# A four-layer state-space network: who scales the inflows of the scans, who forms the C products, and when the next chunk is prepared

## The chip, the core and the metric

The kernel runs on one core of a Trainium2 chip. Five engines have a queue of instructions each and run it in order: TensorE (PE; its weight loads are shown as PEld) multiplies and transposes into PSUM, VectorE (DVE), ScalarE (ACT) and GpSimd (POOL) work element by element, and SyncE (SP) issues the transfers. Engines wait for each other by semaphores. The metric is the time of one execution on the device in microseconds; lower is better.

## The reference

Four layers are applied to four images of 64 x 64 pixels with 192 channels. Each normalizes its input by groups, projects it, convolves it, and runs selective scans over it. Layer 0 ("a" in the kernel) has four directions over single rows or columns, each 64 long; layer 1 ("b") one direction, layer 2 ("c") four with 192 channels, layer 3 ("d") four with 384, all over the whole image of 4096 positions. The core of all is the recurrence, here from layer 3:

```python
def step(hst, inp):
    d, bm, cm, uu = inp
    dA = jnp.exp(d[..., None] * A[None])
    dBu = (d * uu)[..., None] * bm[:, :, None, :]
    hst = dA * hst + dBu
    y = jnp.einsum('bkdn,bkn->bkd', hst, cm)
    return (hst, y)
...
delta = jax.nn.softplus(dts + dt_projs_bias[None, :, :, None])
ys = ys + xs * Ds.reshape(K, D_INNER)[None, :, :, None]
```

There are 16 states n for every channel d. Four things are computed for each: the decay dA, the inflow dBu (delta times u, times B), the scan itself, and the product with C, which is summed over the states. All arithmetic is in 32-bit floats.

## The kernel before

**Tiling.** `scans` (from line 313 on) handles all scans of one layer. The sequence is cut into chunks of T = 512 positions. A chunk has 384 channels as nb = 3 blocks of 128 partitions; the 16 states are taken as 8 pairs j of NT = 2. One tile is one pair of one block, 128 x 1024 elements, so a chunk has 24 tiles and each tile has one scan on VectorE (line 695). In c the rows and columns are worked on side by side in one set of blocks (`ways` = 2). For an image a has 32 chunks, b 8, c 16 and d 32.

**Steps.** The loop at line 800 runs over all tiles, one tile a step s, and writes the order of each engine's queue by hand: `keep` (line 437) ties each instruction behind the one before it on its engine. In step s the queues get: the decays of tile s+3 (two exponentials on ScalarE, line 631; NF = 4 buffers in a, b, d and 3 in c), the inflow of tile s+1, the scalings due in this step, the scan of tile s, loads for later tiles, the C product of tile s-1 on GpSimd or of tile s on VectorE (line 710), and the sum of tile s-3 (or s-1 after VectorE) by transposing matmuls into one PSUM bank a block (`total`, line 750). So the inflow of tile s+1 stands in TensorE's queue in front of the totals and of the preparation of step s.

**Inflows.** There are four ways to form dBu. "p": GpSimd multiplies du by a broadcast B (line 637), and the decay lies in PSUM. The other three work on du transposed (duT, positions on partitions, where B is one number a partition). "t": ScalarE scales duT by B (line 658), TensorE transposes the result into PSUM (line 674). "g": the same with GpSimd scaling (line 651). "d": TensorE multiplies duT by a diagonal matrix that holds B (line 670); the matrix is written element by element into memory and loaded again as D. `WAYS` gives order and way of the pairs: in a three pairs d, four t, one g; in b and d two d, two g, four t; in c p and t in turn. PSUM holds two inflow tiles ("ps"); a buffer is free when the scan has read it, or, where VectorE makes the C product in place, after that product.

**C products.** `PRODUCTS` says for each of a chunk's 24 tiles whether GpSimd ("p", the scan writes to an h buffer in SBUF) or VectorE ("d", the scan writes over its input) forms the product.

**Scalings.** The eight scalings of a pair (two states, four blocks of 128 positions) are laid over the steps ahead of its first tile, 6 steps for t and 9 for g (lines 771 to 777), into three buffers for t and two for g, one buffer a state.

**Preparation.** While a chunk is scanned the next is prepared at the steps of the table `at` (line 552): px (projection to dt, B, C on TensorE, steps 3 to 5), dbl (copy by ScalarE, step 6), pd and pre (delta's projection and bias by block, in one PSUM bank in turn, steps 7 to 11), softplus (12), du on GpSimd (13), the transposes of du and their copies (15 to 20). A `brought` part adds the state carried over a chunk's border through f (lines 501, 680) in b, c and d. In d and the second pass of c the sum of the directions so far is loaded as "far" at step 12 and added by TensorE with the last totals (line 757).

## Time and profile before

Three runs took 30,927.73, 30,931.62 (the median) and 30,941.47 us. The profiled execution took 30,932.74 us with a span of 30,931.0 us from the first to the last instruction; the granted TensorE clock was 0.945 of full speed on the mean.

| engine | busy us | share of the span | instructions |
|---|---|---|---|
| TensorE, matmuls | 26,989.1 | 87% | 183,112 |
| TensorE, weight loads | 21,403.1 | 69% | 183,112 |
| VectorE | 24,057.7 | 78% | 14,749 |
| ScalarE | 22,386.5 | 72% | 42,791 |
| GpSimd | 22,167.3 | 72% | 13,662 |

The DMA engines were busy for 35.5% of the span with the kernel's own queue. In the profile a group of instructions is shown as "line engine operation out<-in shapes xcount | busy us, mean ns of one | idle time of the engine just before them, and what ended it"; names end in the layer's letter. A line of waits reads "engine, tile and line <- what released it: us in total, times, longest". Busy time of TensorE counts modelled ends of pipelined matmuls, so a busy TensorE need not be at its peak. A releaser is inferred from the last semaphore, and with several waits it can be another than the one named. The four images repeat the same pattern, so one image's layers show the stages.

### The profile page before, as it was taken

Reading aid. Unit: us, or ns where it says so; the run is one execution under the profiler, and the core shown is the slowest. Engines: PE = TensorE matmul, PEld = TensorE weight load, DVE = VectorE, ACT = ScalarE, POOL = GpSimd, SP = SyncE. Lnnn points to the kernel's source line nnn. Section 1 sums busy time; section 2 is a strip of 40 time slices with the busy share of each in tenths; the row PEclk is TensorE's granted clock in tenths of the full one; section 3 lists DMA queues with packets and bytes.
Section 4 is the critical chain, followed back from the end, with each engine's and each line's share of the span. In section 5 each row is a group of like instructions: output and inputs, shape, how many; then the busy total and the mean of one; then the engine's idle time right before and its main releaser. Section 6 shows DMA issues by size and latency. Waiting matters only on the chain. (4 is left out here: it accounts for less than half of the span.)

```text
span 30931.0 us, 474683 instructions
## 1 busy us (share of the span) xinstructions
PE 26989.1 (87%) x183112; PEld 21403.1 (69%) x183112; DVE 24057.7 (78%) x14749; ACT 22386.5 (72%) x42791; POOL 22167.3 (72%) x13662
## 2 busy tenths in 40 slices
PE   8998877999899986799989988779998998877998
PEld 6885655887688565588768856558876885655886
DVE  7884788887788478888778847888877884788887
ACT  6883686886688368688668836868866883686886
POOL 4882686887588268688758826868875882696897
PEclk9999988999999998899999999889999999988999
DMA  3332343333333234333333323433333332343333
GB/s 114 108 109 80 88 116 100 92 99 102 108 109 108 81 87 115 102 92 100 102 108 108 108 81 88 115 102 92 100 103 108 109 109 78 89 115 101 91 100 100
DMA packets 2029473, 3108.17 MB, mean 100 GB/s; under 512 B 902744, under 2 KB 1350600, under 8 KB 2019272
## 3 DMA queue, kind: packets, MB, share of 16 engines
q1 hardware_dynamic: 2027208, 3077.78, 35.5%
q8 instruction: 1444, 23.66, 0.3%
q14 instruction: 821, 6.73, 0.1%
HBM read 2590.78 MB, written 486.54 MB: 99 GB/s over the span
## 5 line engine op out<-in xcount | busy, mean ns | idle before, releaser
L710 POOL TENSOR_TENSOR c_a<-h_a,C_a 128x1024 f32<-128x1024 f32 x2688 | 6334.4, 2373 | 1555.4 <-DVE h_a L695 874.0
L695 DVE TENSOR_TENSOR_SCAN h_d<-dAs_d,carry_d,ut_d 128x1024 f32<-128x1024 f32 x2688 | 6198.1, 2336 | 1417.1 <-PE ut_d L670 854.1
L710 POOL TENSOR_TENSOR c_d<-h_d,C_d 128x1024 f32<-128x1024 f32 x2688 | 6390.9, 2384 | 1040.0 <-PE py_d L750 454.8
L695 DVE TENSOR_TENSOR_SCAN h_a<-dAs_a,ut_a 128x1024 f32<-128x1024 f32 x2688 | 6008.0, 2273 | 1042.7 <-POOL dut_a L651 301.0
L631 ACT ACTIVATE dAs_a<-delta_a,A_a 128x504 f32<-128x504 f32 x6144 | 4039.0, 707 | 1083.8 <-DVE h_a L695 772.7
L631 ACT ACTIVATE dAs_d<-delta_d,A_d 128x512 f32<-128x512 f32 (+1 forms) x6144 | 4093.1, 715 | 653.6 <-DVE h_d L695 496.4
L750 PE MATMUL py_a<-ident,c_a 128*128 128x128 f32 x24576 | 3195.0, 277 | 11.1 <-DVE c_a L710 11.1
L750 PE MATMUL py_d<-ident,c_d 128*128 128x128 f32 x24576 | 3153.3, 273 | 11.2 <-DVE c_d L710 11.2
L674 PE MATMUL ut_d<-ident,dut_d 128*128 128x128 f32 x18432 | 2893.3, 281 | 306.2 <-DVE c_d L710 133.3
L674 PEld LDWEIGHTS ut_d<-ident,dut_d 128*128 128x128 f32 x18432 | 2201.2, 152 | 1173.7 <-DVE h_d L695 374.9
L750 PEld LDWEIGHTS py_a<-ident,c_a 128*128 128x128 f32 x24576 | 2840.3, 143 | 12.1 <-DVE c_a L710 12.1
L750 PEld LDWEIGHTS py_d<-ident,c_d 128*128 128x128 f32 x24576 | 2793.1, 142 | 66.2 <-issue 53.8
L750 PE MATMUL py_c<-ident,c_c 128*128 128x128 f32 x12288 | 1915.8, 313 | 936.3 <-DVE c_c L710 689.7
L674 PE MATMUL ut_a<-ident,dut_a 128*128 128x128 f32 x15360 | 2148.9, 283 | 564.9 <-ACT dut_a L658 387.2
L674 PEld LDWEIGHTS ut_a<-ident,dut_a 128*128 128x128 f32 x15360 | 1739.2, 144 | 1087.6 <-ACT dut_a L658 419.9
L750 PEld LDWEIGHTS py_c<-ident,c_c 128*128 128x128 f32 x12288 | 1666.9, 163 | 1142.0 <-DVE c_c L710 669.9
L670 PEld LDWEIGHTS ut_a<-D_a,duT_a 128*128 128x128 f32 x18432 | 2144.9, 192 | 365.2 <-DVE h_a L695 253.3
L670 PE MATMUL ut_a<-D_a,duT_a 128*128 128x128 f32 x18432 | 2280.0, 278 | 103.7 <-DVE c_a L710 75.9
L710 POOL TENSOR_TENSOR c_c<-h_c,C_c 128x1024 f32<-128x1024 f32 x960 | 2254.8, 2364 | 152.9 <-issue 106.8
L658 ACT ACTIVATE dut_d<-duT_d,BT_d 128x384 f32<-128x384 f32 x4096 | 2321.0, 603 | 0.7 <-PE ut_d L674 0.7
L658 ACT ACTIVATE dut_a<-duT_a,BT_a 128x384 f32<-128x384 f32 x4096 | 2316.2, 601 | 0.9 <-PE ut_a L674 0.7
L695 DVE TENSOR_TENSOR_SCAN h_c<-dAs_c,carry_c,ut_c 128x1024 f32<-128x1024 f32 x768 | 1766.9, 2335 | 167.5 <-PE ut_c L674 157.5
(374 smaller groups left out, 54166.5 us busy)
## 6 DMA issues: line engine op xcount, KB each, us to landing
C_a<-bc_a SPq DMA_DIRECT2D x1024, 512.0 KB
C_d<-bc_d SPq DMA_DIRECT2D x1024, 512.0 KB
C_c<-bc_c SPq DMA_DIRECT2D x1024, 256.0 KB
D_a<-dg SPq DMA_DIRECT2D x384, 512.0 KB
C_b<-bc_b SPq DMA_DIRECT2D x256, 512.0 KB
B_c<-bc_c SPq DMA_DIRECT2D x512, 256.0 KB
D_d<-dg SPq DMA_DIRECT2D x256, 512.0 KB
xd_a<-xo_a SPq DMA_DIRECT2D x48, 2048.0 KB
```

The source lines that it names most:

```text
L631: keep(nc.scalar.activation(out, delta, AF.Exp, scale=o.A[:, t.b, k : k + 1]))
L658: keep(nc.scalar.activation(o[:, :, g, :], i[:, :, g, :], AF.Copy, scale=c.BT[:, q, g, n : n + 1]))
L670: keep(nc.tensor.matmul(out, t.c.duT[:, q, blk], t.c.D[t.j][:, n, q, :], start=q == 0, stop=stop))
L674: keep(nc.tensor.matmul(out, t.c.scaled[t.n0 + n][:, q, blk], self.ident, start=q == 0, stop=stop, is_transpose=True,))
L695: keep(nc.vector.tensor_tensor_scan(hf, af, uf, initial, ALU.mult, ALU.add))
L710: keep(engine.tensor_tensor(t.cm, t.h, t.c.C[t.j], ALU.mult))
L750: keep(nc.tensor.matmul(c.py[b][:, q, :], t.cm[:, n, q * 128 : (q + 1) * 128], self.ident[:P, :P], start=first, stop=last and q == TB - 1 ...
```

## The change

All inflows take the form with duT; the way "p" with its loads of B, its u tiles and its decays in PSUM is gone. In a five pairs are scaled by ScalarE, two by GpSimd and one is diagonal; in b and d five and three, with no diagonal; in c four and four. The pairs now run in their natural order 0 to 7. GpSimd's scaling of c works on half-blocks, 128 x 192 elements, two instructions for each state and block of positions. VectorE forms 4 C products a chunk in a, 5 in b and d, 8 in c. The scalings of a chunk are spread evenly from step -7 (t) or -6 (g) of a chunk to two steps before the last such pair is used, with four buffers for t, and three (four in c) for g. The decays have four buffers in all layers, h five. The table of the preparation is packed into steps 0 to 17, and the sum so far is loaded into the tile that the result will be stored from. Only C goes through memory to be broadcast.

```diff
-WAYS = {
-    0: ((2, "d"), (0, "t"), (3, "d"), (1, "t"), (5, "g"), (6, "t"), (4, "d"), (7, "t")),
-    1: ((3, "d"), (0, "t"), (2, "g"), (1, "t"), (4, "d"), (6, "t"), (5, "g"), (7, "t")),
-    2: tuple((j, "pt"[j % 2]) for j in range(8)),
-}
-DIAGS = {0: (4, 6), 1: (6, 4)}
-ROW = 3328
+WAYS = {0: "tgttgttd", 1: "tgttgttg", 2: "tgtgtgtg"}
+DIAGS = {0: (14, 2)}
+ROW = 1280
...
-PRODUCTS = {1: "pppppppdpppppppdpppppppd", 2: "dpdpppdpdpppdddpppdpdppp"}
+PRODUCTS = {
+    0: "pppppdpppppdpppppdpppppd", 1: "ppppdppppdppppdppppdpppd", 2: "ppdppdppdppdppdppdppdppd",
+}
+FIRST_SCALE = {"t": -7, "g": -6}
...
-        HB = 5 if ways == 1 else 4
-        DUT = {"t": 3, "g": 2}
-        AHEAD = {"t": 2 * nb, "g": 3 * nb}
...
-            c.bc = dp.tile([ways, 2 * NS, T], F32, tag="bc", bufs=3, name=f"bc_{c.key}")
+            c.bc = dp.tile([ways, NS, T], F32, tag="bc", bufs=3, name=f"bc_{c.key}")
             for g in range(ways):
-                k = g * (DR + 2 * NS) + DR
-                keep(nc.sync.dma_start(c.bc[g], c.dbl[k : k + 2 * NS, :]))
-            if ways == 1:
+                k = g * (DR + 2 * NS) + DR + NS
+                keep(nc.sync.dma_start(c.bc[g], c.dbl[k : k + NS, :]))
+            if kind in DIAGS:
...
-            c.du = sp.tile([P, nb, T], F32, tag="du", bufs=ways, name=f"du_{c.key}")
+            c.du = sp.tile([P, nb, T], F32, tag="du", bufs=1, name=f"du_{c.key}")
...
-            0: [p_dir], 3: [p_px(0)], 4: [p_px(1)], 5: [p_px(2)], 6: [p_dbl, p_const],
-            7: [p_pd(0)], 8: [p_pre(0)], 9: [p_pd(1)], 10: [p_pre(1), p_pd(2)], 11: [p_pre(2)],
-            12: [p_softplus, p_turn_B], 13: [p_du, p_BT, p_first],
+            0: [p_dir], 3: [p_px(0)], 4: [p_px(1), p_px(2)], 5: [p_dbl, p_const], 6: [p_pd(0)],
+            7: [p_pre(0), p_pd(1)], 8: [p_pre(1), p_pd(2)], 9: [p_pre(2)],
+            10: [p_softplus, p_turn_B], 11: [p_du, p_BT, p_first], 13: [p_turn_du(0)],
+            14: [p_duT(0), p_turn_du(1)], 15: [p_duT(1), p_turn_du(2)], 16: [p_duT(2)],
+            17: [p_brought],
         }
...
-            if t.turned:
-                t.dA = fixed[t.turn % NF]
-            else:
-                t.dA = pp.tile([P, NT, T], F32, tag="ps", bufs=2, name=f"dA_{t.key}")
+            t.dA = fixed[t.turn % NF]
...
-            if not t.turned:
-                keep(nc.scalar.copy(starts, zeros if short else zeros[:, 0]))
-
-        def inflow(t):
-            t.u = sp.tile([P, NT, T], F32, tag="u", bufs=3, name=f"u_{t.key}")
-            keep(nc.gpsimd.tensor_tensor(
-                t.u, t.c.du[:, t.b, None, :].to_broadcast([P, NT, T]), t.c.B[t.j], ALU.mult
-            ))
-            if not short:
-                u = t.u[:, second(t.c), first(t.c)][:, None]
-                keep(nc.gpsimd.tensor_tensor(u, u, t.c.f[:, t.j, t.b : t.b + 1], ALU.add))
         def scaled(c, n, q, way):
             if q == 0:
                 c.scaled[n] = sp.tile(
-                    [128, TB, nb * P], F32, tag="dut" if way == "t" else "dug", bufs=DUT[way],
-                    name=f"dut_{c.key}_{n}",
+                    [128, TB, nb * P], F32, tag=f"du{way}", bufs=4 if way == "t" else 2 + ways,
+                    name=f"du{way}_{c.key}_{n}",
                 )
-            if way == "g":
-                keep(nc.gpsimd.tensor_scalar(
-                    c.scaled[n][:, q, :], c.duT[:, q, :], c.BT[:, q, 0, n : n + 1], 1.0,
-                    ALU.mult, ALU.mult,
-                ))
-                return
             o, i = (x[:, q, :].rearrange("p (b g c) -> p b g c", b=nb, g=ways) for x in (c.scaled[n], c.duT))
             for g in range(ways):
-                keep(nc.scalar.activation(
-                    o[:, :, g, :], i[:, :, g, :], AF.Copy, scale=c.BT[:, q, g, n : n + 1]
-                ))
-
-        def turned_inflow(t):
+                o_, i_, B = o[:, :, g, :], i[:, :, g, :], c.BT[:, q, g, n : n + 1]
+                if way == "t":
+                    keep(nc.scalar.activation(o_, i_, AF.Copy, scale=B))
+                else:
+                    keep(nc.gpsimd.tensor_scalar(o_, i_, B, 1.0, ALU.mult, ALU.mult))
...
-                t.h = sp.tile([P, NT, T], F32, tag="h", bufs=HB, name=f"h_{t.key}")
+                t.h = sp.tile([P, NT, T], F32, tag="h", bufs=5, name=f"h_{t.key}")
-                [P, NT, T], F32, tag="cp" if t.pool_c else "c", bufs=3 if t.pool_c else ways,
+                [P, NT, T], F32, tag="cp" if t.pool_c else "c", bufs=3 if t.pool_c else 1,
...
+            c.yt = sp.tile([128, TB, nb * P], F32, tag="yt", bufs=1, name=f"yt_{c.key}")
             if c.o.so_far is not None:
-                c.far = sp.tile([128, TB, nb * P], F32, tag="far", bufs=1, name=f"far_{c.key}")
+                c.far = c.yt
...
-        for k, t in enumerate(tiles):
-            if t.way in "tg" and t.b == 0:
-                ops = [(t.c, t.n0 + n, q, t.way) for n in range(NT) for q in range(TB)]
-                steps = range(k - AHEAD[t.way], k - 1)
-                for i, op in enumerate(ops):
-                    scales.setdefault(max(steps[i * len(steps) // len(ops)], -1), []).append(op)
+        for n, c in enumerate(chunks):
+            for way in "tg":
+                pairs = [j for j in range(NS // NT) if WAYS[kind][j] == way]
+                ops = [(j, j * NT + k, q) for j in pairs for k in range(NT) for q in range(TB)]
+                for i, (j, k, q) in enumerate(ops):
+                    step = FIRST_SCALE[way] + i * (nb * pairs[-1] - 2 - FIRST_SCALE[way]) // len(ops)
+                    step = n * per_chunk + min(step, nb * j - 2)
+                    scales.setdefault(max(step, -1), []).append((c, k, q, way))
```

The loop itself then has, in each step, the decays of tile s+3, the inflow of tile s+1, the scalings, and the rest as before.

## The prediction

> **What bounds the kernel now.** I read the busy shares first: TensorE 87%, VectorE 78%, ScalarE and GpSimd 72% each, so no engine is full, and the average cannot say what binds. Then I split by stage: the stretches from the first to the last scan of layers a, b, c and d in the first of the four images (time, busy time of five engines, granted clock).
>
> ```profile
> core 0: us, PE busy (x) PEld busy (x) DVE busy (x) ACT busy (x) POOL busy (x), PEclk, DMA share, GB/s
> 314.90:2525.60 2210.70, 2041.61 (x16188) 1807.47 (x16187) 1834.15 (x869) 1796.04 (x3009) 1831.75 (x962) 0.98 0.36 106
> 3080.00:3629.00 549.00, 516.78 (x4186) 458.53 (x4184) 469.14 (x238) 453.23 (x909) 489.84 (x320) 0.99 0.29 84
> 3921.70:5066.30 1144.60, 838.98 (x5624) 719.00 (x5624) 1059.72 (x673) 1051.29 (x2453) 1091.48 (x682) 0.86 0.44 114
> 5332.80:7601.60 2268.80, 2144.48 (x16516) 1821.00 (x16515) 1883.12 (x958) 1848.87 (x3701) 1998.07 (x1310) 0.99 0.34 94
> ```
>
> With 32, 8, 16 and 32 chunks of 24 scans a chunk takes 69.1 us in a, 68.6 in b, 71.5 in c, 70.9 in d. VectorE is idle for 11.8, 10.0, 5.3 and 12.0 us of them. In c GpSimd works 68.2 of 71.5 us: c is bound by GpSimd. In a, b and d somebody makes VectorE wait; the table of waits says who (first two lines from a's stretch, the last two from d's: total, times, longest).
>
> ```profile
> DVE h_a L695 <- PE ut_a L670: 82.4, 46, 30.9
> DVE ut_a L695 <- PE ut_a L670: 68.9, 31, 2.4
> ...
> DVE h_d L695 <- PE ut_d L670: 223.0, 151, 25.1
> ACT e_d L495 <- POOL e_d L491: 116.1, 31, 6.4
> ```
>
> L670 is the inflow of the pairs marked "d" (duT by a diagonal matrix). Without the first wait of the layer it costs a (82.4-30.9+68.9)/32 = 3.8 us a chunk and d (223.0-25.1)/32 = 6.2. The order of time in chunk 4 of a shows how:
>
> ```profile
> 612.44 2.05 PE L670 MATMUL ut_a<-D_a,duT_a 128*128 128x128 f32 x16
> 614.33 1.06 PE L741 MATMUL py_a<-dgD_a,xs_a 128*128 128x128 f32 x8
> 614.63 2.29 DVE L695 TENSOR_TENSOR_SCAN h_a<-dAs_a,ut_a 128x1024 f32<-128x1024 f32 x1 [2.45 <-POOL dut_a L651]
> 615.22 1.04 PE L750 MATMUL py_a<-ident,c_a 128*128 128x128 f32 x8
> 616.19 1.05 PE L440 MATMUL px_a<-xs_a,xw_a 128*44 128x512 f32 x2
> 617.17 2.05 PE L670 MATMUL ut_a<-D_a,duT_a 128*128 128x128 f32 x16
> 617.28 0.58 ACT L447 COPY dbl_a<-px_a 44x512 f32<-44x512 f32 x1 [2.73 <-PE px_a L440]
> 623.74 1.09 PE L674 MATMUL ut_a<-ident,dut_a 128*128 128x128 f32 x8
> ```
>
> TensorE needs 4.73 us from inflow to inflow and VectorE stands 2.45 us: the scan began when L670 ended (the releaser printed is only the last semaphore). A diagonal inflow is 16 passes (1.89 us to the next start), a transposed one 8 (0.95 by the same spacing). So TensorE binds in the steps where the next chunk's preparation joins in.
>
> **The change, engine by engine, per chunk.** Durations are from these groups (count, busy us, mean ns):
>
> ```profile
> L695 DVE TENSOR_TENSOR_SCAN h_d<-dAs_d,carry_d,ut_d 128x1024 f32<-128x1024 f32 x2688 | 6198.1, 2336 | 1417.1 <-PE ut_d L670 854.1 <-PE ut_d L674 496.7 <-ACT dAs_d L631 45.1
> L637 POOL TENSOR_TENSOR u_c<-du_c,B_c 128x1024 f32<-128x1024 f32 x768 | 1823.0, 2374 | 0.0
> L651 POOL TENSOR_SCALAR dut_d<-duT_d,BT_d 128x384 f32<-128x384 f32 x2048 | 1234.1, 606 | 18.8 <-ACT duT_d L545 18.8
> L642 POOL TENSOR_TENSOR u_c<-u_c,f_c 128x1 f32<-128x1 f32 x768 | 147.0, 191 | 60.2
> L710 DVE TENSOR_TENSOR c_d<-ut_d,C_d 128x1024 f32<-128x1024 f32 x384 | 466.3, 1214 | 0.0
> L631 ACT ACTIVATE dAs_c<-delta_c,A_c 128x512 f32<-128x512 f32 x768 | 547.7, 713 | 0.0
> L631 ACT ACTIVATE dA_c<-delta_c,A_c 128x512 f32<-128x512 f32 x768 | 530.4, 691 | 114.6 <-DVE h_c L695 90.5 <-DVE c_c L710 11.2
> ```
>
> - VectorE: C products go from 3 to 4 in a, 3 to 5 in b and d, 9 to 8 in c, each 1.21 to 1.22 us and in b, c, d a carry copy of 0.16 (L703). Busy time: a 57.3+1.2 = 58.5; b 58.6+2.7 = 61.3; d 58.8+2.7 = 61.5; c 66.2-1.4 = 64.8. This lies on the path: VectorE runs every scan in turn.
> - ScalarE: 8 more scalings in a, b, d, 0.57 us each (2316.2/4096): +4.5, so a 60.6, b 61.2, d 62.3. In c 12 start copies of 0.16 go (-1.9) and 24 exponentials write SBUF rather than PSUM. Singly that is 691 ns into PSUM and 713 into SBUF, but two in a row take 1.39 to 1.42 us into PSUM and 1.33 into SBUF in c's first chunk, about 0.70 against 0.62 from start to start, so 24 x -0.08 = -1.9 and c is 65.7-3.8 = 61.9. [...]
> - GpSimd: a loses one product (2.36) and gains 8 scalings of 0.59: 57.2+2.3 = 59.5. b and d lose 2 products, gain 8: 61.2 and 62.4, unchanged. In c 12 inflow products with their additions (2.37+0.19) go, -30.7; one C product comes, +2.35; and 64 scalings of 128x192 come that no row has. Bounds: 0.19 (one element, L642) and 0.60 (384, L651), 12 to 38 us. I take the half-way value by size, 0.39, 25 us: c 68.2-30.7+2.4+25 = 64.9 (52 to 78).
> - TensorE: 6 diagonal tiles fewer in a, b and d, 0.94 us each, -5.6 us. In c 12 inflows more, +11 to 13 us beside 71.5-52.4 = 19 idle; its clock of 0.86 there can only rise with more work.
> - DMA: B loads of c, all D loads but one pair of a, and the one-element diagonal writes go; the queues were at a third and no row above has VectorE waiting for a load, so 0. The running sum is now loaded into yt, nine steps after yt's store was issued; that store lands 4.6 us later in the chain of waits, so 0. More buffers (h in c, decays in c): 0.
>
> **What stalls remain.** The preparation keeps its work but is packed: two of the px pairs in step 4, pd in 6 to 8 (was 7, 9, 10), softplus in 10 (was 12). In a, TensorE has for steps 3 to 7: 3.8 (inflow 0.95, skip 0.89, total 0.97, px 0.98), 4.8, 2.8, 4.0 (two totals, pd 1.1), 3.0 = 18.4 us; VectorE has 5 x 2.2 (scans start 2.2 apart where nothing waits) + 1.2 = 12.2. TensorE can be about 1.2 ahead: 5.0 lost. Before, for steps 3 to 9: 25.1 against 16.6, 7.3 lost.
>
> A new wait comes in a, b and d. ScalarE's scaled tiles stand in four buffers, two pairs. By the new spread (40 operations over 23 steps from -7) the first of pair 5 is issued in step 6, but needs a buffer of pair 2, whose last inflow is tile 8, in TensorE's step 7. ScalarE waits there, and queued behind it are that scaling (0.5), decay 10 (1.3), two scalings (1.0) and the bias pass pre(0) (0.7): 3.5 us. TensorE's pd(1) waits for pre(0), because both use one bank, and behind pd(1) stands the next inflow: about 3.1 us of VectorE idle in b and d, 2.6 in a, where a total of 0.9 lies beside part of it. Softplus with its two table loads (4 us) and the wait for e (116.1/31 = 3.7 in d) come two steps earlier, with their old distance; decays are made three ahead, so I leave 1.0 to 1.5 for them. In b and d steps 3 to 8, laid out in the same way without the skip, lose 1.0. In d the sum so far (L757, 0.86 a block) still meets the totals of steps 0 and 1: 1.7 lost; by columns the px pair takes 1.9, 2.3 more in half of the chunks.
>
> Idle after, a: 5.0+2.6+1.0 less 1.0 absorbed by ScalarE lagging = 7.6, chunk 66.1 (-3.0). b: 1.0+3.1+1.5 = 5.6, 66.9 (-1.7). d: 1.7+1.0+3.1+1.5+1.1 = 8.4, 69.9 (-1.0). c: bounds VectorE 64.8 and GpSimd 64.9 together, 4 us of waiting, near its present 5.3: 68.8 (-2.7). The start of a layer: the first pair is now scaled by ScalarE, whose 6 decays (4 us) and 8 scalings (4.1) stand ahead of the first inflow; the fourth scan comes about 4 us later, 16 layers, +70.
>
> Sum over 128, 32, 64 and 128 chunks: -384 - 54 - 173 - 128 + 70 = -669. The profiled execution took 30932.7 (span 30931.0 and 1.7 around it), 1 us from the median of 30931.6, so 30,260; the rest, 6,240 us outside the scans, is untouched. **Forecast 30,250**, own range 29,800 to 30,800 (c's scalings between 0.3 and 0.5, the new wait between 1 and 5 us).
>
> **Rivals.**
> - *ScalarE takes the place of the diagonals (slower).* The new wait repeats: pd(1), pd(2) and the decays behind softplus each wait for ScalarE, which is at 62.3 of 70. For it: the waits of ScalarE on dbl (2.73 above) and e already cost 5 us a chunk in d. Against: those waits shrink when ScalarE lags. Price: 4 us more in the 288 chunks of a, b, d, +1,150: 31,400. It decides from 669/288 = 2.3 us a chunk.
> - *GpSimd binds c.* At 0.60 a scaling GpSimd has 78 us there, chunk 80: 64 x 11.2 = 720 more, 30,970, no change. For it: each scaling is a separate dispatch; against: size mattered between L642 and L651.
> - *A larger gain.* The new wait is swallowed by ScalarE's lag and the bursts shrink to 4 us: a 63, b 65.5, c 67.1, d 67: -781-99-282-499+70 = -1,590, 29,340. Against: the tight steps 3 to 8.
>
> **How the numbers follow.** Chances: forecast 0.60, ScalarE's place 0.20, GpSimd in c 0.08, larger gain 0.12. A difference under 0.2% (62 us) can't be told from none. The forecast and the larger gain are faster, 0.72 together; the GpSimd case lies about no change and is split 0.05 same, 0.03 slower; with ScalarE's 0.20 that is 0.23 slower. The range reaches down to half of the larger gain and up to half of the slower case: 29,500 to 31,150.
>
> **What would show it.** L670 left in a alone, at a third of its count; no wait on it in d; ScalarE's first dut of pair 5 waiting for TensorE by 3 to 5 us and pd waiting for delta; c's GpSimd busy near 65 of 69 us with scalings near 0.39; scans of 2.27 to 2.34 us unchanged. A scaling over 0.5 us in c, or ScalarE idle under 3 us a chunk in a or d with VectorE idle above 11, would prove the forecast wrong.

## The result and the profile after

The changed kernel took 32,773.6 us (median of four runs, 32,756.8 to 32,790.4), the kernel before 30,929.7 on the same chip: a ratio of 1.0596, 95% interval 1.0578 to 1.0614. It is 6.0% slower, where the prediction had 2.2% faster. The profiled execution has a span of 32,755.0 us. Now and then an execution of the same kernel is slower at a lower clock (30,453 us at 0.905 instead of 30,014 at 0.959 for one of the kernels below), so for kernels that ran once a difference of a few hundred microseconds needs the waits and the clock of its profile beside it.

The same view as before, the stretches from the first to the last scan of a, b, c and d in the first image (start and end; length; busy time of five engines; granted clock, DMA share, GB/s):

```profile
core 0: us, PE busy (x) PEld busy (x) DVE busy (x) ACT busy (x) POOL busy (x), PEclk, DMA share, GB/s
316.50:2574.10 2257.60, 1967.84 (x14660) 1712.44 (x14658) 1869.10 (x901) 1895.63 (x3250) 1894.36 (x1178) 0.93 0.29 89
3135.90:3744.40 608.50, 506.57 (x3810) 442.18 (x3808) 487.99 (x270) 475.99 (x945) 488.45 (x365) 0.92 0.19 63
4046.60:5278.70 1232.10, 1004.73 (x7532) 916.67 (x7530) 1043.81 (x639) 1003.98 (x2252) 1065.87 (x1321) 0.91 0.29 79
5550.80:8037.00 2486.20, 2076.25 (x14988) 1742.93 (x14986) 1960.82 (x1086) 1966.06 (x3880) 1996.12 (x1499) 0.92 0.23 72
```

A chunk takes 70.6, 76.1, 77.0 and 77.7 us: +1.5, +7.4, +5.5 and +6.8 (the first column of lengths over 32, 8, 16 and 32 chunks). The busy times of VectorE, ScalarE and GpSimd are what the prediction said, to within 2 us a chunk. What is wrong is the idle time: VectorE stands idle for 12.1, 15.1, 11.8 and 16.4 us a chunk instead of 7.6, 5.6, 4 and 8.4, while no other engine is full. And TensorE, with less to do, has a lower clock: 0.92 in d, where it had 0.99.

The table of waits in d's stretch (engine, tile and line, what released it; us in total, times, longest):

```profile
DVE h_d L656 <- PE ut_d L635: 306.5, 187, 31.1
...
ACT dut_d L619 <- PE ut_d L635: 137.0, 32, 5.1
DVE ut_d L656 <- PE ut_d L635: 128.0, 29, 4.9
...
PE td_d L533 <- ACT duT_d L540: 98.1, 31, 3.2
PE pd_d L459 <- ACT delta_d L467: 92.8, 31, 3.0
...
ACT duT_d L540 <- PE td_d L533: 81.9, 31, 3.3
```

Before the change TensorE hardly waited at the same two places of d, pd behind pre and td behind duT:

```profile
PE pd_d L464 <- ACT delta_d L472: 8.8, 31, 0.3
...
PEld td_d L538 <- ACT duT_d L545: 0.2, 1, 0.2
```

The waits for diagonals are gone. In their place stand three, each 2.6 to 4.3 us in every chunk but one at most. The second line is the wait for the ring of scaled tiles that the prediction named (4.3 us a chunk), the fifth what it does to pd (3.0). The fourth and the last are TensorE and ScalarE waiting for each other over td and duT, the transposes of du and their copies out of one PSUM bank: the prediction has no price for them. VectorE then waits for ut, the inflow. By step (start of a scan to start of the next, mean over the chunks): in b and d 4.3 us are lost before scan 9, 3.0 and 3.5 before scan 16, 1.9 and 1.8 before scan 17; in c 2.9 and 1.3 before scans 16 and 17; in a 5.8 us before scans 9 to 11 and 1.2 before 16 and 17. (Scans are counted from 0 in a chunk, as the steps are.)

The order of time in chunk 4 of d shows the hand-over. These lines of that stretch are in order; L533 is td, L540 its copy duT, L635 the inflow, L712 the totals, L607 decays, L619 scalings:

```profile
5914.74 1.33 ACT L607 ACTIVATE dAs_d<-delta_d,A_d 128x512 f32<-128x512 f32 x2
5915.15 2.34 DVE L656 TENSOR_TENSOR_SCAN h_d<-dAs_d,carry_d,ut_d 128x1024 f32<-128x1024 f32 x1
5915.98 1.10 ACT L619 ACTIVATE dut_d<-duT_d,BT_d 128x384 f32<-128x384 f32 x2
...
5917.07 0.57 ACT L540 COPY duT_d<-td_d 128x512 f32<-128x512 f32 x1
...
5917.69 1.12 PE L533 MATMUL td_d<-ident,du_d 128*128 128x128 f32 x4 [3.22 <-ACT duT_d L540]
...
5918.60 1.06 PE L635 MATMUL ut_d<-ident,dut_d 128*128 128x128 f32 x4
...
5919.74 1.09 PE L635 MATMUL ut_d<-ident,dut_d 128*128 128x128 f32 x4
...
5920.63 3.34 PE L712 MATMUL py_d<-ident,c_d 128*128 128x128 f32 x16
5920.97 2.35 DVE L656 TENSOR_TENSOR_SCAN h_d<-dAs_d,carry_d,ut_d 128x1024 f32<-128x1024 f32 x1 [3.49 <-PE ut_d L635]
...
5923.80 0.60 PE L533 MATMUL td_d<-ident,du_d 128*128 128x128 f32 x4
5924.24 0.60 PE L635 MATMUL ut_d<-ident,dut_d 128*128 128x128 f32 x4
5924.44 0.59 ACT L540 COPY duT_d<-td_d 128x512 f32<-128x512 f32 x1 [3.26 <-PE td_d L533]
...
5924.82 0.64 PE L635 MATMUL ut_d<-ident,dut_d 128*128 128x128 f32 x4
```

ScalarE has no gap here; its copy duT(0) comes behind decays and scalings at 5917.07. TensorE has td(1) at the head of its queue and stands 3.22 us for that copy, and behind td(1) stands the inflow of the next scan, which needs nothing of it. VectorE loses 3.49 us. Then td, the inflow and the totals run at half speed (td 1.12 instead of 0.60 us, four inflow passes 1.06 instead of 0.60), td(2) comes late by that, and ScalarE now waits 3.26 us for it. The granted clock of three stretches of 6 us around this (columns as above):

```profile
5911.60:5917.60 6.00, 2.60 (x23) 2.12 (x20) 5.85 (x5) 6.00 (x15) 6.00 (x5) 0.93 0.28 87
5917.60:5923.60 6.00, 5.91 (x29) 5.91 (x30) 2.35 (x1) 3.58 (x8) 5.54 (x5) 0.51 0.24 87
5923.60:5929.60 6.00, 5.38 (x51) 5.15 (x50) 4.01 (x2) 4.55 (x9) 4.60 (x4) 1.00 0.00 0
```

### The profile page after: what moved, and what is told of

Read it like the earlier page. It is cut to its first block, busy times and chain, and to the rows that moved or that the text cites. A ratio compares the mean times of both kernels' runs of the same rounds, so it can differ in the third digit from the quotient of the medians.

```text
span 32755.0 us, 467671 instructions
## 1 busy us (share of the span) xinstructions
PE 27104.5 (83%) x176968; PEld 21471.4 (66%) x176968; DVE 24527.1 (75%) x15389; ACT 23277.8 (71%) x44079; POOL 22330.5 (68%) x18142
## 5 line engine op out<-in xcount | busy, mean ns | idle before, releaser
L671 POOL TENSOR_TENSOR c_a<-h_a,C_a 128x1024 f32<-128x1024 f32 x2560 | 6055.6, 2377 | 1472.0 <-PE py_a L712 935.3
L671 POOL TENSOR_TENSOR c_d<-h_d,C_d 128x1024 f32<-128x1024 f32 x2432 | 5765.0, 2371 | 1855.1 <-DVE h_d L656 933.1
L656 DVE TENSOR_TENSOR_SCAN h_d<-dAs_d,carry_d,ut_d 128x1024 f32<-128x1024 f32 x2432 | 5612.3, 2336 | 1679.4 <-PE ut_d L635 1230.9
L656 DVE TENSOR_TENSOR_SCAN h_a<-dAs_a,ut_a 128x1024 f32<-128x1024 f32 x2560 | 5709.0, 2272 | 1317.2 <-PE ut_a L635 857.2
L607 ACT ACTIVATE dAs_d<-delta_d,A_d 128x512 f32<-128x512 f32 (+1 forms) x6144 | 4088.8, 713 | 503.1 <-DVE h_d L656 457.5
L607 ACT ACTIVATE dAs_a<-delta_a,A_a 128x504 f32<-128x504 f32 x6144 | 4048.1, 707 | 456.0 <-DVE h_a L656 387.1
L712 PE MATMUL py_d<-ident,c_d 128*128 128x128 f32 x24576 | 3345.2, 286 | 91.1 <-POOL c_d L671 77.6
L619 ACT ACTIVATE dut_a<-duT_a,BT_a 128x384 f32<-128x384 f32 x5120 | 2887.2, 603 | 592.7 <-PE ut_a L635 592.7
L619 ACT ACTIVATE dut_d<-duT_d,BT_d 128x384 f32<-128x384 f32 x5120 | 2883.6, 602 | 548.2 <-PE ut_d L635 548.2
L712 PE MATMUL py_a<-ident,c_a 128*128 128x128 f32 x24576 | 3254.8, 281 | 7.8 <-DVE c_a L671 7.8
L712 PEld LDWEIGHTS py_d<-ident,c_d 128*128 128x128 f32 x24576 | 3017.6, 150 | 172.4 <-POOL c_d L671 103.0
L635 PE MATMUL ut_d<-ident,dut_d 128*128 128x128 f32 x15360 | 2646.3, 302 | 418.1 <-DVE c_d L671 202.8
L712 PEld LDWEIGHTS py_a<-ident,c_a 128*128 128x128 f32 x24576 | 2919.6, 146 | 8.8 <-DVE c_a L671 8.8
L635 PEld LDWEIGHTS ut_d<-ident,dut_d 128*128 128x128 f32 x15360 | 2029.1, 165 | 1099.9 <-issue 715.6
L656 DVE TENSOR_TENSOR_SCAN h_c<-dAs_c,carry_c,ut_c 128x1024 f32<-128x1024 f32 x1024 | 2355.9, 2333 | 373.8 <-PE ut_c L635 352.6
L635 PE MATMUL ut_a<-ident,dut_a 128*128 128x128 f32 x15360 | 2316.0, 300 | 348.3 <-DVE c_a L671 300.0
L635 PEld LDWEIGHTS ut_a<-ident,dut_a 128*128 128x128 f32 x15360 | 1943.5, 155 | 912.5 <-issue 759.5
L607 ACT ACTIVATE dAs_c<-delta_c,A_c 128x512 f32<-128x512 f32 (+1 forms) x3072 | 2044.8, 714 | 472.3 <-DVE h_c L656 349.8
L656 DVE TENSOR_TENSOR_SCAN ut_d<-dAs_d,carry_d,ut_d 128x1024 f32<-128x1024 f32 x640 | 1493.9, 2334 | 547.4 <-PE ut_d L635 513.8
L621 POOL TENSOR_SCALAR dug_d<-duT_d,BT_d 128x384 f32<-128x384 f32 x3072 | 1798.7, 592 | 115.6 <-PE ut_d L635 96.8
L712 PE MATMUL py_c<-ident,c_c 128*128 128x128 f32 x12288 | 1774.8, 301 | 11.9 <-DVE c_c L671 11.9
```

The source lines that it names most:

```text
L607: keep(nc.scalar.activation(out, delta, AF.Exp, scale=o.A[:, t.b, k : k + 1]))
L619: keep(nc.scalar.activation(o_, i_, AF.Copy, scale=B))
L621: keep(nc.gpsimd.tensor_scalar(o_, i_, B, 1.0, ALU.mult, ALU.mult))
L635: keep(nc.tensor.matmul(out, t.c.scaled[t.n0 + n][:, q, blk], self.ident, start=q == 0, stop=stop, is_transpose=True,))
L656: keep(nc.vector.tensor_tensor_scan(hf, af, uf, initial, ALU.mult, ALU.add))
L671: keep(engine.tensor_tensor(t.cm, t.h, t.c.C[t.j], ALU.mult))
```

## The experiments

My first theory was the table: TensorE and ScalarE pass one bank back and forth in consecutive steps, plus the ring wait. The rival was the load: five pairs and all decays on ScalarE leave it too little slack wherever the preparation stands. All times per chunk below are means over the four images (before 69.1, 68.7, 71.5, 70.6 in a, b, c, d; after 70.5, 76.1, 77.2, 77.9), and a kernel that ran once is compared by that one time.

| kernel | us | a | b | c | d |
|---|---|---|---|---|---|
| before, packed table alone | 31,163 | 69.6 | 68.2 | 75.0 | 70.4 |
| changed, old table, first scalings at -3 | 29,989 | 64.0 | 66.8 | 71.2 | 68.1 |
| changed, td spread, -5 | 30,763 | 66.3 | 69.5 | 72.6 | 70.5 |
| changed, pd spread and td later, -5 | 30,698 | 67.0 | 68.2 | 71.5 | 70.1 |
| changed, -5 alone | 32,176 | 69.8 | 73.4 | 77.1 | 74.6 |
| changed, -3 alone | 32,123 | 69.0 | 72.3 | 79.2 | 74.2 |
| changed, pair 5 later | 31,914 | 69.5 | 71.2 | 77.3 | 73.4 |
| the same, copies first | 31,839 | 69.6 | 70.4 | 77.2 | 73.1 |
| changed, pd and td behind the inflow | 31,581 | 68.2 | 71.4 | 74.5 | 73.5 |
| the same, pair 5 later | 31,050 | 67.9 | 69.1 | 74.3 | 70.3 |
| changed, td two steps later, -5 | 31,033 | 66.6 | 68.9 | 73.4 | 72.0 |
| changed, TensorE kept busy | 32,127 | 70.2 | 72.4 | 77.6 | 74.1 |
| old table, -3, pair 5 later | 30,014 | 64.0 | 66.8 | 71.4 | 68.2 |
| old table, -3, C products as before | 29,954 | 64.6 | 66.1 | 71.3 | 67.4 |

**The old table in the changed kernel.** The scalings need all of duT, so they can't begin at -7 where duT is ready at step 20; they begin at -3.

```diff
-FIRST_SCALE = {"t": -7, "g": -6}
+FIRST_SCALE = {"t": -3, "g": -3}
...
-            0: [p_dir], 3: [p_px(0)], 4: [p_px(1), p_px(2)], 5: [p_dbl, p_const], 6: [p_pd(0)],
-            7: [p_pre(0), p_pd(1)], 8: [p_pre(1), p_pd(2)], 9: [p_pre(2)],
-            10: [p_softplus, p_turn_B], 11: [p_du, p_BT, p_first], 13: [p_turn_du(0)],
-            14: [p_duT(0), p_turn_du(1)], 15: [p_duT(1), p_turn_du(2)], 16: [p_duT(2)],
-            17: [p_brought],
+            0: [p_dir], 3: [p_px(0)], 4: [p_px(1)], 5: [p_px(2)], 6: [p_dbl, p_const],
+            7: [p_pd(0)], 8: [p_pre(0)], 9: [p_pd(1)], 10: [p_pre(1), p_pd(2)], 11: [p_pre(2)],
+            12: [p_softplus, p_turn_B], 13: [p_du, p_BT, p_first], 15: [p_turn_du(0)],
+            16: [p_duT(0)], 17: [p_turn_du(1), p_brought], 18: [p_duT(1)], 19: [p_turn_du(2)],
+            20: [p_duT(2)],
```

> The changed kernel with the preparation of the next chunk spread over steps 3 to 20 as before the change (a step of the table between ScalarE's copy out of a PSUM bank and TensorE's next use of that bank), and the first scalings at step -3 instead of -7 and -6, since duT is ready only by step 20. Theory P (the packed table: TensorE and ScalarE hand one PSUM bank back and forth within one step, so each hand-over waits for the decays and scalings queued ahead of it): the idle of 3 to 4 us a chunk before scans 8 to 10 and of 4 to 5 us before scans 15 to 17 goes, in its place up to 2 us a chunk where the eight scalings of pair 0 are squeezed into two steps; 30,400 to 31,200 us, b, c and d at 69 to 72 us a chunk. Rival R (the load itself: five pairs and the decays on ScalarE leave it too little slack, wherever the preparation stands): 32,400 to 33,100 us, no chunk shorter by more than 1 us.

Measured: 29,988.8, below the lower end of what the theory gave. Run again, in turn with the kernel before:

> The run with the old table and first scalings at -3 again, timed against the kernel before: 29,988.8 us once, so 3.0% under it; 29,950 to 30,030 us.

29,997.2 us (29,992.0 to 30,010.5) against 30,936.8: a ratio of 0.9697, 95% interval 0.9680 to 0.9713. So the change without its packed table and early scalings is 3.0% faster than the kernel before, and 8.5% faster than with them. The same windows of that kernel's timed run, a and d:

```profile
315.50:2362.40 2046.90, 1860.31 (x14660) 1598.67 (x14658) 1864.24 (x901) 1890.35 (x3249) 1891.41 (x1178) 1.00 0.32 98
...
5173.90:7355.00 2181.10, 1968.22 (x14988) 1636.35 (x14986) 1951.69 (x1086) 1956.09 (x3879) 1989.56 (x1499) 0.98 0.26 82
```

VectorE, ScalarE and GpSimd have the busy times of the changed kernel to 0.5% (d: 1,952, 1,956 and 1,990 us against 1,961, 1,966 and 1,996). The load is the same and the stretch of d is 305 us shorter: the rival falls in its plain form.

**The packed table in the kernel before.** The hunk of the table above, the other way round, in the kernel before; nothing else.

> The kernel before, with the new table of the preparation alone (px of two blocks in step 4, pd, pre, td and duT in consecutive steps, all by step 16); ways, products and scalings as before. P: each of the two chains costs its stall here too, about 3 us a chunk at pd/pre and 4 to 5 us at td/duT where a chunk of b, c and d has three blocks: before + 1,300 to 2,300 us. R: ScalarE has less to do here than in the changed kernel and takes the hand-overs up: within 1% of before (30,620 to 31,240 us).

31,163.4 us, +0.8%: the rival's number, not the theory's. In the main c lost (+3.5 us a chunk); a lost 0.5, b and d gained 0.5 and 0.2. The waits for the two banks in d:

```profile
PEld td_d L538 <- ACT duT_d L545: 32.7, 61, 0.9
...
PE td_d L538 <- ACT duT_d L545: 17.3, 45, 0.7
```

A matmul of td waits 0.7 us at the longest for duT (its weight load 0.9), against 3.2 in the changed kernel, and TensorE's clock in d is 1.00. So the packed table alone is not enough: it costs 242 us here, and, as the runs below show, some 2,100 in the changed kernel. In chunk 4 of this kernel the copy duT(0) ends 1.6 us before the scan in progress does, in the changed kernel (5917.64) 0.15 us after it (5917.49). Two things differ: ScalarE has 32 scalings a chunk here and 40 there (by the two tables 1 and 0 in steps 13 and 14 here, 2 and 2 there), and TensorE, which has diagonals here, comes to td(1) later itself. Which of them counts more was not separated.

**Half of the table spread.** td and duT in steps 13 to 18, or pd and pre in 6 to 11 with td packed in 15 to 18; both with first scalings at -5.

```diff
-            14: [p_duT(0), p_turn_du(1)], 15: [p_duT(1), p_turn_du(2)], 16: [p_duT(2)],
+            14: [p_duT(0)], 15: [p_turn_du(1)], 16: [p_duT(1)], 17: [p_turn_du(2), p_brought],
+            18: [p_duT(2)],
```

> The changed kernel with td and duT alone spread out again: steps 13 to 18, each block's transposes one step after the copy of the block before; first scalings at step -5. P: the idle of 4 to 5 us a chunk before scans 15 to 17 of b, c and d goes (in a, under 1 us), the idle around scans 5 to 10 stays: 31,400 to 31,900 us. R: 32,500 to 33,000 us.

```diff
-            7: [p_pre(0), p_pd(1)], 8: [p_pre(1), p_pd(2)], 9: [p_pre(2)],
-            10: [p_softplus, p_turn_B], 11: [p_du, p_BT, p_first], 13: [p_turn_du(0)],
-            14: [p_duT(0), p_turn_du(1)], 15: [p_duT(1), p_turn_du(2)], 16: [p_duT(2)],
+            7: [p_pre(0)], 8: [p_pd(1)], 9: [p_pre(1)], 10: [p_pd(2)], 11: [p_pre(2)],
+            12: [p_softplus, p_turn_B], 13: [p_du, p_BT, p_first], 15: [p_turn_du(0)],
+            16: [p_duT(0), p_turn_du(1)], 17: [p_duT(1), p_turn_du(2), p_brought], 18: [p_duT(2)],
```

> The changed kernel with pd and pre alone spread out (steps 6 to 11), softplus in step 12, du in 13, td and duT packed as in the change but two steps later (15 to 18); first scalings at step -5. P: the idle of 3 to 4 us a chunk before scans 8 to 10 shrinks to about 1 us, since ScalarE's wait at step 6 for the ring of scaled tiles (4.3 us a chunk) then meets fewer hand-overs; the idle at td/duT stays: 31,600 to 32,200 us. R: 32,500 to 33,000 us.

30,763 and 30,698: each gave back about 2,000 us of 2,785 and lies below the range that the theory gave. Stalls that I had assigned to the other half went too. The two runs share the later first scalings, so these were tried alone, with the packed table untouched.

> The changed kernel with its packed table untouched, and only the first scalings moved: step -5 for both engines instead of -7 and -6. Theory F (the early first scalings: from -7 on, pair 5's first scaling stands in step 6, where its ring buffer is still read by pair 2, and the scalings crowd steps 13 to 17, where ScalarE and TensorE hand the bank over): the ring wait falls from 4.3 us a chunk of b and d to under 2, most of the stalls before scans 9, 16 and 17 go; 30,700 to 31,300 us. Theory T (the packed table itself is what stalls, whatever the scalings do): above 32,000 us.

> The changed kernel with its packed table untouched, and the first scalings at step -3, as in the run with the old table, from which it differs in the table alone. Theory F: the packed table alone costs what it costs in the kernel before, 0 to 2 us a chunk of a, b and d and about 4 of c, 100 to 900 us; 30,100 to 30,900 us. Theory T: above 31,800 us.

32,176 and 32,123: the first scalings are worth 600 to 650 us, not 2,000, and the table makes the rest. The kernel with -3 differs from the one of 29,989 in the table alone: 2,134 us. Theory F falls. With -3, c is even worse (79.2): 5.2 us are lost before scans 16 and 17 instead of 4.2, and 32 scalings lie on 19 steps instead of 23; that the one follows from the other was not tested.

**Where td stands among the scalings.** The packed table with td and duT moved as a block from steps 13 to 16 to steps 15 to 18, first scalings at -5 (compare 32,176).

```diff
-            14: [p_duT(0), p_turn_du(1)], 15: [p_duT(1), p_turn_du(2)], 16: [p_duT(2)],
+            16: [p_duT(0), p_turn_du(1)], 17: [p_duT(1), p_turn_du(2), p_brought], 18: [p_duT(2)],
```

> The changed kernel with first scalings at step -5 (the run of that alone took 32,176 us) and td and duT packed as in the change but two steps later, in steps 15 to 18, where ScalarE has 1, 0, 0, 0 scalings instead of 2, 2, 1, 0 in steps 13 to 16; pd and pre packed as in the change. If scalings ahead of the copies make them late: the stall before scans 16 to 18 falls from 5.4 to under 2 us a chunk of d, 30,800 to 31,500 us. If packing alone does it: within 300 us of 32,176.

31,033, within the range expected of scalings that make the copies late, and 1.1 us a chunk of d are left before scans 16 to 18. Consecutive steps cost little where the copy ends early enough. The waits in d of this kernel:

```profile
PEld td_d L533 <- ACT duT_d L540: 32.6, 51, 1.2
...
PE td_d L533 <- ACT duT_d L540: 18.2, 22, 1.0
```

18.2 us where the kernel with -5 alone has 114.0. What differs is when the copy ends. On the mean over the chunks of d, duT(0) ends 2.8 us after the start of the next step's scan in the changed kernel, 3.5 us with -5 alone, and 1.1 us here and in the kernel before with the packed table. td(1) and the inflow then take 1.7 us at full clock and a scan 2.3, so by these figures (an estimate) the next scan comes late as soon as the copy ends more than 0.6 us after the start.

ScalarE is not later at this place of d than it was: in the kernel before the copy ends 2.5 us after the start of that scan, in the changed kernel with the old table 2.9. But there td(1) stands a step further on, and TensorE waits 0.0 and 1.0 us for the copy instead of 3.2. What the packed table took away is the step that absorbed the lateness. (In a and c the copy is later than before the change, by 1.4 and 2.7 us; with the old table it is as late or nearly so, and the waits are 0.3 us.)

**The ring wait.** Pair 5's scalings on ScalarE wait in the table, not at the buffer, so that nothing queues behind them.

```diff
+                    if way == "t" and kind < 2 and j == 5:
+                        step = max(step, 8)
                     step = n * per_chunk + min(step, nb * j - 2)
```

> The changed kernel, table and first scalings untouched, but pair 5's scalings on ScalarE (a, b and d) not before step 8, when pair 2's ring buffer has been read; c, whose pairs on ScalarE are 0, 2, 4 and 6, is the same. The ring wait (137 us of 2,486 in the first d) goes. If that wait is the cause of the stall before scan 9: b and d 3 to 4.5 us a chunk shorter, a 2 to 4, c unchanged at 77; 31,500 to 32,100 us. If the stall is the packed pd and pre alone, it stays: 32,500 to 32,900 us.

31,914: -860 us, b and d -4.9 and -4.5 us a chunk, a -1.0, c unchanged, as expected but for a. In d the wait of 137.0 us is gone, that of pd is down from 92.8, and td's stays:

```profile
PE td_d L533 <- ACT duT_d L540: 99.9, 31, 3.2
...
PE pd_d L459 <- ACT delta_d L467: 10.2, 28, 0.4
```

In a the 5.8 us before scans 9 to 11 fell to 1.7, but the loss before scans 16 and 17 rose from 1.2 to 4.4: the wait for the ring had hidden most of a's loss at td. The step and mechanism of the prediction are shown, a little dearer than its 3.1 us. In the kernel with the old table the same edit gave nothing:

> The run with the old table and first scalings at -3, with pair 5's scalings on ScalarE not before step 8 as well. The ring wait that is left there (1.4 us a chunk before scan 5 to 6 of a, little in b and d) goes: 29,750 to 29,980 us. If that wait only hides the next one: 29,980 to 30,050.

30,014 us (ratio 0.9697, 0.9677 to 0.9716), the same as without it. The expectation had read a wait of VectorE for a late scaling, 1.4 us a chunk of a before scan 5, as the ring's. ScalarE has no wait for TensorE at the scalings of a there; with first scalings at -3 the ring is no longer met, and the 1.7 us before scan 5 of a stay.

**ScalarE's copies first.** As the run with pair 5 later; pre and duT are issued ahead of the step's scalings (behind its decays).

```diff
+        early = {7: [p_pre(0)], 8: [p_pre(1)], 9: [p_pre(2)], 14: [p_duT(0)], 15: [p_duT(1)], 16: [p_duT(2)]}
...
+            if t and t.c.n + 1 < len(chunks):
+                for f in early.get(s - t.c.n * per_chunk, []):
+                    f(chunks[t.c.n + 1])
             for op in scales.get(s, []):
                 scaled(*op)
```

> As the run with pair 5's scalings later, and ScalarE's copies out of the handed-over bank (pre in steps 7 to 9, duT in 14 to 16) are placed ahead of the step's scalings and decays instead of behind them; TensorE's side of the packed table is untouched. If the copies' place behind the scalings is what keeps TensorE waiting at td and duT: the stalls before scans 16 and 17 (5 us a chunk in b and d, 4 in c) shrink to under 2 us, 900 to 1,600 us below the run with pair 5 later alone. If not (TensorE's own queue ahead of td, or the decays made late by the copies): within 300 us of it.

31,839, 75 us below it: a miss for the theory. In d the copy duT(0) ends 3.0 us after the start of scan 15 instead of 3.5, and the scalings behind it were late: 2.0 us a chunk of VectorE's idle time before scan 16 now ends with ScalarE's dut. Here another order of ScalarE's own queue moved the loss and did not remove it, which points to what ScalarE had left over from the steps before, and not to the scalings of the copy's own step.

**TensorE's place in the queue.** Copies and scalings in their steps; pd(1), pd(2), td(1) and td(2) behind the next inflow instead of ahead of it; then the same with pair 5 later.

```diff
-            7: [p_pre(0), p_pd(1)], 8: [p_pre(1), p_pd(2)], 9: [p_pre(2)],
+            7: [p_pre(0)], 8: [p_pre(1)], 9: [p_pre(2)],
...
+        mid = {8: [p_pd(1)], 9: [p_pd(2)], 15: [p_turn_du(1)], 16: [p_turn_du(2)]}
...
             if s + 1 < N:
                 inflow(tiles[s + 1])
+            if t and t.c.n + 1 < len(chunks):
+                for f in mid.get(s - t.c.n * per_chunk, []):
+                    f(chunks[t.c.n + 1])
```

> The changed kernel with every copy and every scaling in its step; only TensorE's pd and td of blocks 1 and 2 are moved in its queue, from ahead of the next step's inflow to behind it. Theory Q (the wait for ScalarE's copy itself is harmless; what costs is the inflow of the next scan queued behind it, and the half-clock matmuls that follow a wait of over 3 us): the stalls before scans 16 and 17 go and that before scan 9 shrinks to about 1 us, d at 69.5 to 71.5 us a chunk, c at 71 to 73, a at 67 to 69, TensorE's clock in d back above 0.96; 30,300 to 31,300 us. Rival L (ScalarE is too late in steps 8 and 14 to 16 in any case, so the next decays and scalings are late too): above 32,000 us.

> The same, and pair 5's scalings on ScalarE not before step 8 (no wait for the ring of scaled tiles). Theory Q: what is left before scans 5 to 9 falls by another 0.5 to 2 us a chunk of a, b and d: 100 to 500 us below the run without it. If TensorE's place in the queue has already hidden the ring wait: within 60 us of it.

31,581 and 31,050. The first is 1,192 us better than the changed kernel, but 281 above the range that the theory gave: the losses before scans 9 and 16 went entirely in d, but 3.0 us stand before scan 17 (1.8 in the changed kernel) and 1.0 to 1.5 before each of scans 10 to 12, where the next of the chain is late. The second is 531 us below the first, a little more than the 100 to 500 expected, so the ring wait was not hidden. In it the largest wait of VectorE in d is for ScalarE itself:

```profile
DVE h_d L656 <- ACT dAs_d L607: 162.2, 82, 3.3
DVE h_d L656 <- PE ut_d L635: 145.3, 119, 31.3
```

With td(1) and td(2) behind the inflow, 3.2 us a chunk of d are lost before scan 17, and 2.2 of them end with a decay of ScalarE. To that extent the rival holds: at this place, not on the average.

**The half clock by itself.** The order is left as the change has it. Ten matmuls by zeros are put at each of the two places where TensorE stands and waits anyhow; they add nothing to the sum.

```diff
+        def p_warm(c):
+            if c.n:
+                py = chunks[c.n - 1].py[0]
+                for k in range(10):
+                    keep(nc.tensor.matmul(
+                        py[:, k % TB, :], self.ident[:P, :], zeros[:, 0, 0:1].to_broadcast([P, P]),
+                        start=False, stop=False,
+                    ))
...
-            7: [p_pre(0), p_pd(1)], 8: [p_pre(1), p_pd(2)], 9: [p_pre(2)],
+            7: [p_pre(0), p_warm, p_pd(1)], 8: [p_pre(1), p_pd(2)], 9: [p_pre(2)],
...
-            14: [p_duT(0), p_turn_du(1)], 15: [p_duT(1), p_turn_du(2)], 16: [p_duT(2)],
+            14: [p_duT(0), p_warm, p_turn_du(1)], 15: [p_duT(1), p_turn_du(2)], 16: [p_duT(2)],
```

> The changed kernel, order and table untouched, with ten matmuls of a 128x128 identity by zeros, added to the running sum py and so adding nothing to the result, on TensorE right ahead of pd(1) and of td(1): about 2.2 us of work (20 passes of about 0.11 us) in a place where TensorE otherwise stands for 3.0 to 3.2 us in b and d. Theory H (the half clock that follows those waits is a cause of its own: in d's chunk 4 it makes td 1.12 us instead of 0.60, the inflow 2.2 instead of 1.6, the 16 totals 3.34 instead of 2.1, and td(2) late by as much): TensorE's clock in d goes from 0.92 to above 0.97, the stalls before scans 16 and 17 of b and d shrink from 5 to 2 or 3 us, c by 2, a by 0 to 1; 31,700 to 32,300 us. Rival: the clock makes no difference beside ScalarE's lateness, or the added work costs what the clock gives: 32,600 to 33,100 us.

32,126.6: 647 us less, with more work. d in the first image, and the stretches of 6 us around the same place of chunk 4:

```profile
5512.20:7880.00 2367.80, 2088.53 (x16228) 1767.61 (x16226) 1959.04 (x1086) 1962.34 (x3880) 1994.42 (x1499) 0.99 0.24 76
```
```profile
5862.10:5868.10 6.00, 6.00 (x58) 6.00 (x57) 5.87 (x5) 6.00 (x15) 6.00 (x5) 1.00 0.27 87
5868.10:5874.10 6.00, 5.39 (x51) 5.15 (x49) 4.86 (x3) 4.76 (x10) 6.00 (x6) 1.00 0.26 87
5874.10:5880.10 6.00, 4.39 (x38) 3.95 (x39) 5.96 (x5) 6.00 (x13) 6.00 (x7) 1.00 0.26 87
```

The clock of d is back at 0.99 and in chunk 4 the 16 totals take 1.91 us instead of 3.34. The waits for td in d:

```profile
PE td_d L533 <- ACT duT_d L540: 29.1, 30, 1.0
...
ACT duT_d L540 <- PE td_d L533: 13.6, 31, 0.6
```

The first was 98.1, but that is no gain: the ten matmuls (2.4 us in chunk 4) stand in the wait, and the copy duT(0) ends 2.9 us after the start of scan 15, no earlier than before (2.8). The second was 81.9, and that is the clock: td(2) is no longer late. The loss before scan 9 of d fell from 4.3 to 2.9 us, before scan 16 from 3.5 to 2.4, before scan 17 from 1.8 to 0.9. b and d gained 3.7 and 3.8 us a chunk, a and c next to nothing (2 us had been expected in c): a gained 2.9 before scans 9 to 11 and lost 2.6 before scans 16 and 17, as in the run with pair 5 later. The ring wait is untouched (137.0). So the half clock is a cause of its own, about a third (647 of 1,844 us) of what was lost against the kernel before; the other two thirds are lost without it.

**The shares of the C products.** The kernel with the old table, products as before the change.

> The run with the old table and first scalings at -3, with the C products shared out as before the change (VectorE 3 in a, b and d, 9 in c; the rest on GpSimd). VectorE has 1.2 us a chunk less in a, 2.7 less in b and d, 1.4 more in c; GpSimd 2.4 more in a, 4.7 more in b and d (67 of 68 us), 2.4 less in c. If GpSimd's load then binds b and d: 30,000 to 30,500 us. If VectorE's own work is what bounds the good schedule: 29,500 to 29,900.

29,954, 0.14% below 29,997, which is no difference that can be told, and between the two ranges expected. a lost 0.6 us a chunk, b and d gained 0.7 to 0.8, c is the same. VectorE's and GpSimd's shares weigh alike here, and moving products to VectorE neither helped nor hurt.

## Why the prediction was wrong, point by point

**Right: the loads.** VectorE is busy 58.4, 61.0, 65.2 and 61.3 us a chunk (forecast 58.5, 61.3, 64.8, 61.5), ScalarE 59.2, 59.5, 62.7 and 61.4 (60.6, 61.2, 61.9, 62.3), GpSimd 59.2, 61.1, 66.6 and 62.4 (59.5, 61.2, 64.9, 62.4). The scaling of 128x192, for which no row had a price, is in this group:

```profile
L621 POOL TENSOR_SCALAR dug_c<-duT_c,BT_c 128x192 f32<-128x192 f32 x4096 | 1677.5, 431 | 18.8 <-ACT duT_c L540 18.8
```

1677.5/4096 = 0.41 us against the estimate of 0.39; the rival in which GpSimd binds c falls. ScalarE in c has 62.7 against 61.9 by the spacing, on which the sum went. By the durations of single exponentials, 691 ns into PSUM and 713 into SBUF, it would have been about 64.3 (an estimate: 61.9 without the 1.9 saved and with 24 x 0.022 more): the measured time is nearer to what the time from start to start gave. TensorE's 5.6 us a chunk of diagonals is right too, but shows only where the clock holds: a has 63.8 us before (clock 0.98), 61.5 in the changed kernel (0.93) and 58.1 with the old table (1860.31/32, at 1.00).

**Right in kind, too small: the new wait.** "ScalarE waits there ... TensorE's pd(1) waits for pre(0), because both use one bank, and behind pd(1) stands the next inflow" is what the trace shows, 4.3 to 4.7 us at the ring, and at pd 3.0 in b and d and 2.2 in a. It cost 4.3 us before scan 9 in b and d instead of 3.1, and 5.8 before scans 9 to 11 in a instead of 2.6. The term was mis-sized because the steps behind the wait ran at half clock (0.50 for 6.8 us from 5,892.8 in chunk 4 of d, where pd waited 3.00 us for pre), at which no term of the sum was reckoned: with TensorE kept busy 2.6 and 2.9 us are lost there in b and d, and 2.9 in a.

**The step that failed: "The preparation keeps its work but is packed".** The prediction laid TensorE's work out over steps 3 to 8 and said of softplus and the wait for e that they come "two steps earlier, with their old distance"; of td and duT it said nothing, which put them at no cost. They did not keep their distance: they went from every second step to every step. That is 4.9 and 5.3 us a chunk in b and d, 4.2 in c and 1.2 in a (4.4 in a once the ring wait is gone). The same kind of wait had been worked out for pd just before, and the chain td(1) behind duT(0) on one bank has the same shape. Beneath it lies the second omission: ScalarE's work was summed by chunk (62 of 70 us) and not laid out by step, so nothing said when the copy ends. In d it ends 2.8 us after the start of scan 15; with the 1.7 us of td(1) and the inflow, less a scan of 2.3, scan 16 comes 2.2 us late at full clock. Measured were 2.4 us with TensorE kept busy, and 3.5 without.

**c.** "4 us of waiting, near its present 5.3" had no working behind it: 11.8 were measured. 4.2 are td's, and 4.0 lie before scans 2 and 5; the old table takes c to 71.2, about where it was. What keeps it from the forecast 68.8 is idle time, 6.1 us a chunk instead of 4, of which 2.2 stand before scan 5, where VectorE waits for the inflow; why that comes late was not looked into. TensorE's clock in c rose from 0.86 to 0.91, with 1,004.73 us of matmuls in the stretch instead of 838.98.

**The layer's start.** The 16 gaps ahead of the first scans of the layers grew by 113 us together, forecast +70.

**The sum.** The idle time beyond the forecast is 4.5, 9.5, 7.8 and 8.0 us a chunk; over 128, 32, 64 and 128 chunks that is 576 + 304 + 499 + 1,024 = 2,403, and 43 from the layer starts: 2,446 of the 2,524 us between 30,250 and 32,774.

**The rivals.** "ScalarE takes the place of the diagonals" was right in its mechanism (pd and the decays wait for ScalarE) and in its sign, but the price was 4 us in a, b and d only; excess idle was 4.5 to 9.5, in c as well, and in b, c and d half of it or more came through td, which the rival did not name. Its 31,400 lies 1,374 us too low. Its sign of recognition, a ScalarE without idle time, was wrong too: ScalarE is idle for 11 to 17 us a chunk. The larger gain (63, 65.5, 67.1, 67) is near what the same loads give with the old table, 64.0, 66.8, 71.2, 68.1.

## What to carry to other kernels

Where two engines pass one PSUM bank back and forth, price each hand-over by what stands ahead of the copy on the one engine and behind the wait on the other, at the step where it happens; a mean load of 62 in 70 us says nothing about it. An in-order queue turns a harmless wait into a loss when an urgent instruction stands behind it (here TensorE's 3.22 us at td(1) into 3.49 of VectorE): keep such chains a step apart, or at steps where the copy has little ahead of it. When part of a change packs a schedule and part of it moves load, try the two apart: here the rest of the change was worth 3.0%, and the packing with its early scalings cost 9%.

## What the runs showed of the hardware that was not expected

A stall of TensorE cost twice here. At the wait of 3.2 us shown above the granted clock was 0.50 for 6.8 us (from 5,916.7 to 5,923.5 in chunk 4), while TensorE worked without a gap for the last 5.9 of them; the clock had fallen already 2.2 us after the last matmul. The stretch from td's start to the end of the inflow took 3.14 us at half clock and 1.66 at full clock 6 us later, and 16 totals 3.34 at half clock and 1.91 at full. Twenty passes of useless work, put into each of the two waits of a chunk, made the kernel 2.0% faster.

The trace of the changed kernel holds 814 stretches of half clock (0.50), 361 of them 3.4 us long, 304 of 6.8 and 73 of 10.2, and no clock but full and half. In the 3.4 us before the fall shown TensorE had worked for 1.1, and before all 814 falls for 1.2 on the median, so most came without 3.4 us of idle time ahead. What makes the clock fall was not shown.
